# An LSTM with residual on one core: another assignment of hidden units to partitions, x and output in 16-step blocks, and a reordered setup

## The chip, the cores and the metric

The kernel runs on one core of a Trainium2 chip. The core has a matrix engine (PE, with its weight loads as PEld), a vector engine (DVE), an activation engine (ACT), a general engine (POOL) and a queue engine (SP). SP, ACT and POOL can issue DMA transfers, and sixteen DMA engines carry them out. The metric is the device time of one execution in microseconds (us).

## The reference

An LSTM over T = 512 steps for N = 16 sequences, with D = H = 512. All tensors are float32.

```
xW = einsum("ntd,dg->ntg", x, Wx) + b          # Wx is 512 x 2048
a  = xW[:, t] + h @ Wh                         # Wh is 512 x 2048
i, f, o = sigmoid(a[:, :512]), sigmoid(a[:, 512:1024]), sigmoid(a[:, 1024:1536])
g  = tanh(a[:, 1536:])
c  = f * c + i * g
h  = o * tanh(c)
out[:, t] = x[:, t] + h
```

`h` starts as `cond_1024` and `c` as zero. Every step needs the `h` of the step before.

## The kernel before, in words

**Layout.** The 512 hidden units (and the 512 inputs) are spread over 128 partitions and four chunks. Partition 32j+u and chunk c hold unit 128j+32c+u. So a 128-wide row of x for one (sequence, step) lies in group j as 128 consecutive floats, and a weight row for partition 32j+u and chunk c is row 128j+32c+u of `Wh` or `Wx`. PE works in four column groups j at once: each matmul writes 32 partitions of a PSUM bank, and the right side is a view of the weights (`wx_j`, `wh_j`, `wq_j`, lines 100 to 102) that picks for group j the columns of its 128 units in each of the four gates.

**Setup (lines 339 to 487).** `load_w` (line 128) loads `Wh` by DMAs of 32 partitions x 2 rows of 8 KB, half of them from SP's queue and half from ACT's; then SP issues the first x block and the start state, POOL issues the bias row, the bias copies and half of `Wx`, and SP the other half. `Wh` is split into three half-precision parts `wq` so that the recurrent product can run in float16. `bound` (line 398) finds the largest magnitude for the scale, `scales` makes the scale, and `split(n, k)` works on eighths n of `Wh` in five stages k: on ACT the first part (k=0), the second (k=2) and the third (k=4), on DVE the two remainders (k=1, k=3). While the split runs, `turn_x` (line 162) transposes x for the first three pairs of steps on DVE, `project` (line 167) multiplies two of them by `Wx` on PE into the banks `xb`, sixteen matmuls with zero follow (line 480), and `seed` (line 178) copies a projection into the gate bank. `xb` holds four pairs; three banks get the bias by matmul before the loop, the fourth by `put_bias` in step 0.

**Loop (lines 489 to 523).** Each step issues on PE, in the order written in `STEP_PE`, twelve `products` (line 186; 96 float16 matmuls of 256 columns) and two calls of `project` for the pair after next (8 float32 matmuls of 512 columns, two passes each). DVE and ACT do the gates in the order of `STEP`. In step 0 `first_products` multiplies the start state by float32 `Wh`. Each engine runs its instructions in the order of the program, since all five are scheduled by hand; the order across engines comes from semaphores. x comes in blocks of XB = 8 steps by 8 DMAs on SP (`load_xs`, line 145; 16 partitions x 4 x 512 B each) into four buffers; `residual` (line 324) adds x on POOL, and `put` (line 315) writes a block of 8 steps with 8 DMAs on SP.

Of the kernel before, what the change touches and what calls it, by code (L numbers as in the profile page):

```python
# [7 lines left out]
FP = mybir.dt.float32  # L8
HP = mybir.dt.float16
I32 = mybir.dt.int32  # L10
AF = mybir.ActivationFunctionType
ALU = mybir.AluOpType
PSUM = bass.MemoryType.PSUM

P = 128
Q = 32
XB = 8
LO = 4096.0
# [13 lines left out]
def lstm_residual(ctx: ExitStack, tc: tile.TileContext, x, h0, wx, wh, b, out):  # L32
# [24 lines left out]


    nc = tc.nc
    N, T, D = x.shape  # L60
# [10 lines left out]
    XP = XB // S2  # L71
    NXB = 4
    assert D == H and NJ * Q == P and N == 16 and S2 == 2 and T % XB == 0 and NK == 4

    const = ctx.enter_context(tc.tile_pool(name="const", bufs=1))
    tmp = ctx.enter_context(tc.tile_pool(name="tmp", bufs=3))
    xsp = ctx.enter_context(tc.tile_pool(name="xsp", bufs=4))
    xtp = ctx.enter_context(tc.tile_pool(name="xtp", bufs=3))
# [20 lines left out]

    wx_j = wx_sb.rearrange("p c (g j w) -> p c j g w", g=G, j=NJ)  # L100
    wh_j = wh_sb.rearrange("p c (e g j h u) -> p c e h j g u", e=2, g=2, j=NJ, h=2)
    wq_j = [w.rearrange("p c (g j h u) -> p c h j g u", g=G, j=NJ, h=2) for w in wq]
    bias = const.tile([P, G * P], FP, tag="bias", name="bias")
    mask = const.tile([P, S2], FP, tag="mask", name="mask")
    zero = const.tile([1, G * P], HP, tag="zero", name="zero")
    amax = const.tile([P, NK], FP, tag="amax", name="amax")
    top = const.tile([P, 2], FP, tag="top", name="top")
# [19 lines left out]

    def load_w(dst, w, c0, dmas, parts=1):


        n = G * H // parts
        for j in range(2):
            for q, dma in enumerate(dmas):
                r = w[(2 * q + j) * P + c0 * Q :][: 2 * Q].rearrange("(c u) f -> u c f", u=Q)
                p = slice((2 * q + j) * Q, (2 * q + j + 1) * Q)
                for e in range(parts):
                    a = parts - 1 - e
                    dma.dma_start(  # L138
                        out=dst[p, c0 : c0 + 2, a * n : (a + 1) * n],
                        in_=r[:, :, e * n : (e + 1) * n],  # L140
                    )

    xs = {}

    def load_xs(s, dma=nc.sync):

        xs[s] = xsp.tile([P, XP, P], FP, tag="xs", name=f"xs_{s}")
        for j in range(NJ):
            for r in range(S2):
                p0 = j * Q + r * N  # L150
                dma.dma_start(
                    out=xs[s][p0 : p0 + N],
                    in_=x[:, s * XB + r : (s + 1) * XB : S2, j * P : (j + 1) * P],
                )

# [6 lines left out]
    def turn_x(q):  # L162
        s, i = divmod(q, XP)
        xT[q] = xtp.tile([P, NK, Q], FP, tag="xT", name=f"xT_{q}")
        nc.vector.transpose(xT[q].rearrange("p c m -> p (c m)"), xs[s][:, i])

    def project(q, c):
        for j in range(NJ):
            nc.tensor.matmul(  # L169
                xb[q % NXB][j * Q : (j + 1) * Q],  # L170
                lhsT=xT[q][:, c],
                rhs=wx_j[:, c, j],
                start=False,
                stop=(c == NK - 1),
                skip_group_check=True,
            )
# [137 lines left out]

    def put(s, i0, i1, dmas):
        for j in range(NJ):
            for r in range(S2):
                p0 = j * Q + r * N
                dmas[r % len(dmas)].dma_start(
                    out=out[:, s * XB + S2 * i0 + r : s * XB + S2 * i1 : S2, j * P : (j + 1) * P],  # L320
                    in_=ob[s][p0 : p0 + N, i0:i1],
                )

    def residual(p):
        s, i = divmod(p, XP)
        if i == 0:
            ob[s] = outp.tile([P, XP, P], FP, tag="ob", name=f"ob_{s}")
        hb = work.tile([P, P], FP, tag="hb", name=f"hb_{p}")
        nc.vector.transpose(hb, hs[p].rearrange("p c m -> p (c m)"))  # L329
        nc.gpsimd.tensor_tensor(ob[s][:, i], hb, xs[s][:, i], ALU.add)  # L330
        if p == NP - 1:
            put(s, i, i + 1, [nc.sync, nc.scalar])
        elif p == NP - 2:
            put(s, 0, i + 1, [nc.sync])
        elif i == XP - 1:
            put(s, 0, XP, [nc.sync])

# [5 lines left out]
    ones = const.tile([1, Q], FP, tag="ones", name="ones")  # L343
    for c in (0, 2):
        load_w(wh_sb, wh, c, (nc.sync, nc.scalar))
    load_xs(0)
    nc.vector.memset(zero, 0.0)
    nc.vector.memset(h_in, 0.0)
    nc.vector.memset(ones, 1.0)
    for j in range(NJ):  # L350
        nc.sync.dma_start(out=h_in[j * Q : j * Q + N], in_=h0[:, j * P : (j + 1) * P])
    nc.gpsimd.dma_start(out=brow, in_=b.rearrange("(o f) -> o f", o=1))
    b_j = b.rearrange("(o e g j w) -> j e o g w", o=1, e=2, g=2, j=NJ)
    for j in range(NJ):
        for e in range(2):
            nc.gpsimd.dma_start(
                out=bias[j * Q : (j + 1) * Q, (1 - e) * GU : (2 - e) * GU].rearrange(
                    "p (g w) -> p g w", g=2
                ),
                in_=b_j[j, e].broadcast_to([Q, 2, P]),  # L360
            )
    for c in (0, 2):
        load_w(wx_sb, wx, c, (nc.sync, nc.gpsimd), 2)
    load_xs(1)
# [7 lines left out]
    for h in range(2):  # L372
        for i in range(2):
            nc.gpsimd.memset(parts[h][i], 0.0)
    nc.scalar.activation(warm, mask[0:1, 0:1], AF.Sigmoid)
# [7 lines left out]

    for bank in gates[0] + gates[1] + xb[3:]:
        zeros(bank, True)
    for bank in xb[:3]:
        for e in range(2):
            for j in range(NJ):
                nc.tensor.matmul(
                    bank[j * Q : (j + 1) * Q, (1 - e) * GU : (2 - e) * GU],  # L390
                    lhsT=ones,
                    rhs=brow.rearrange("p (e g j w) -> p e j g w", e=2, g=2, j=NJ)[:, e, j],
                    start=(e == 0),
                    stop=False,
                    skip_group_check=True,
                )

    def bound(c):
        if c == 1:
            junk = tmp.tile([P, G * H], HP, tag="junk", name="junk", bufs=1)  # L400
            nc.scalar.activation(junk, wh_sb[:, c], AF.Abs, accum_out=amax[:, c : c + 1])
        else:
            nc.vector.tensor_reduce(
                amax[:, c : c + 1],
                wh_sb[:, c],
                mybir.AxisListType.X,
                ALU.max,
                apply_absolute_value=True,
            )

    def scales(h):


        nc.vector.tensor_tensor(
            top[:, h : h + 1], amax[:, 2 * h : 2 * h + 1], amax[:, 2 * h + 1 : 2 * h + 2], ALU.max
        )
# [13 lines left out]
    def split(n, k):  # L430
# [18 lines left out]

    NH = 2 * NK  # L450
    bound(0)
    bound(1)
    scales(0)
# [3 lines left out]
    for n in range(NH):  # L457
        if n == 0:
            bound(2)
        if n == 2:  # L460
            bound(3)
            scales(1)
        if n + 1 < NH:
# [5 lines left out]
        if n + 2 < NH:  # L469
            split(n + 2, 0)  # L470
        if n == 3:
            for q in range(3):
                turn_x(q)
            nc.vector.transpose(hT0.rearrange("p c m -> p (c m)"), h_in)
        if n == 4:
            for c in range(NK):
                for q in range(2):
                    project(q, c)

            for _ in range(16):  # L480
                zeros(xb[3], False)
        if n == 6:
            for h in range(2):
                seed(0, h)
    split(NH - 1, 4)
    for h in range(2):
        seed(1, h)

    for t in range(T):
# [25 lines left out]
        else:  # L515
            if q + 1 < NP:
                put_bias(q + 1)
# [35 lines left out]
```

## Time and profile before

| | us |
|---|---|
| three runs | 2282.47, 2284.65, 2285.02 (median 2284.65) |
| the profiled execution's own time | 2284.45 |
| its span, first to last instruction | 2282.3 |
| first gate transpose of step 0 (DVE, L228) starts | 57.06 |
| distance from one step to the next in the loop | 4.34 |

A profile line gives the source line, the engine, the operation and the tiles (written <- read) with the number of instructions. In a timeline the first two numbers are the start and the length in us; what stands in brackets is how long the engine was idle before and what ended the idle time. In the table by stretches of time the DMA share is the mean busy share of the sixteen DMA engines (a share slightly over 1 means that their packets overlap), followed by GB/s. PE's instructions are counted twice for float32, as two passes.

### The profile page before, as it was taken

To read this page: it belongs to the slowest core of one execution; us is meant where nothing else is said; L and a number is where in the kernel's file an instruction comes from. 1 tells how busy PE (TensorE), PEld (TensorE's weight loads), DVE (VectorE), ACT (ScalarE), POOL (GpSimd) and SP (SyncE) were. 2 spreads that over 40 slices of the span, in tenths; PEclk is the share of its full clock that TensorE was granted. 3 is DMA by queue.
4 is the path that set the end of the run, shared out by engine and by line. 5 is a ranking of instruction groups with operands and counts; after the bars stand their busy time and mean duration, and the time that the engine had idled before them with its cause. 6 is when DMAs were issued, how large, how long until landed. Compare 5 with 4: busy or idle time off the path is not lost.

```text
span 2282.3 us, 137224 instructions
## 1 busy us (share of the span) xinstructions
PE 2239.7 (98%) x57445; PEld 1515.8 (66%) x57445; DVE 1952.7 (86%) x11813; ACT 1839.5 (81%) x7959; POOL 126.7 (6%) x281
## 2 busy tenths in 40 slices
PE   4999999999999999999999999999999999999997
PEld 2666666666666666666666666666666666666665
DVE  5888888888888888888888888888888888888887
ACT  5888888888888888888888888888888888888887
POOL 1000000000000000000000000000000000000000
PEclk9999999999999999999999999999999999999999
DMA  7000100101001001001001001010010010000000
GB/s 167 13 18 18 22 16 20 22 13 22 22 13 22 21 15 22 18 17 22 16 20 22 14 21 23 13 22 22 14 23 19 16 22 17 19 22 14 22 18 13
DMA packets 85004, 51.09 MB, mean 22 GB/s; under 512 B 17104, under 2 KB 82720, under 8 KB 83872
## 3 DMA queue, kind: packets, MB, share of 16 engines
q1 hardware_dynamic: 83008, 37.82, 7.7%
q8 instruction: 451, 7.39, 1.4%
q0 software_dynamic: 928, 2.37, 0.5%
q10 hardware_dynamic: 448, 2.13, 0.4%
q14 instruction: 169, 1.38, 0.2%
HBM read 25.47 MB, written 16.78 MB: 19 GB/s over the span
## 4 chain that ended last, share of the span: by engine, by line
PE 98%; DMA 2%; DVE 0%; issue 0%; ACTq 0%; POOLq 0%; POOL 0%; SPq 0%
PE gates L192 59%; PE xb L169 39%; DMA wh_sb<-in_L_cond_Wh_dram 1%; DMA xs<-in_x_dram 0%; DMA wx_sb<-in_L_cond_Wx_dram 0%; PE gates L205 0%; PE xb L378 0%; ACTq L138 0%; DVE gt L228 0%; DVE preo L235 0%; DVE pre L235 0%; DVE parts L288 0%; DVE gto L228 0%; POOLq L548 0%; POOL ob L330 0%
## 5 line engine op out<-in xcount | busy, mean ns | idle before, releaser
L192 PEld LDWEIGHTS <-parts 128*32 128x32 f16 x49056 | 1265.0, 96 | 397.6 <-DVE parts L288 300.7
L192 PE MATMUL gates<-wq,parts 128*32 128x256 f16 x49056 | 1428.1, 273 | 4.2 <-DVE parts L288 4.2
L169 PE MATMUL xb<-wx_sb,xT 128*32 128x512 f32 x8192 | 969.5, 593 | 22.5 <-DMA wx_sb<-in_L_cond_Wx_dram 22.5
L228 DVE STREAM_TRANSPOSE gt<-gates 128x192 f32<-128x192 f32 x1024 | 391.9, 383 | 220.0 <-PE gates L192 158.4
L169 PEld LDWEIGHTS xb<-wx_sb,xT 128*32 128x32 f32 x8192 | 240.9, 110 | 344.7 <-issue 319.6
L179 ACT ACTIVATE gates<-xb,mask 128x256 f32<-128x256 f32 x1024 | 450.9, 441 | 2.4 <-PE xb L169 2.4
L262 ACT ACTIVATE gc<-pre 128x32 f32<-128x32 f32 x1022 | 234.4, 229 | 260.0 <-DVE pre L235 247.7
L270 ACT ACTIVATE os<-so,sc 128x32 f32<-128x32 f32 x1024 | 329.3, 322 | 16.7
L292 ACT COPY parts<-parts 128x32 f16<-128x32 f16 x1022 | 214.6, 210 | 131.8 <-DVE parts L288 131.8
L235 DVE SCALAR_TENSOR_TENSOR pre<-gt 128x96 f32<-128x96 f32 x1024 | 253.4, 247 | 0.0
L264 ACT ACTIVATE sif<-pre 128x64 f32<-128x64 f32 x1024 | 245.0, 239 | 0.0
L330 POOL TENSOR_TENSOR ob<-hb,xs 128x128 f32<-128x128 f32 x256 | 116.6, 455 | 2136.9 <-DVE hb L329 1816.5
L228 DVE STREAM_TRANSPOSE gto<-gates 128x64 f32<-128x64 f32 x1024 | 229.8, 224 | 0.0
L280 ACT ACTIVATE tch<-gc 128x32 f32<-128x32 f32 x1024 | 227.0, 222 | 0.2
L268 ACT ACTIVATE so<-preo 128x32 f32<-128x32 f32 x1024 | 226.6, 221 | 0.0
L302 DVE SCALAR_TENSOR_TENSOR parts<-rem,parts 128x32 f16<-128x32 f32 x1022 | 196.1, 192 | 35.5
L235 DVE SCALAR_TENSOR_TENSOR preo<-gto 128x32 f32<-128x32 f32 x1024 | 192.2, 188 | 17.4
L294 DVE SCALAR_TENSOR_TENSOR parts<-parts,hist 128x32 f16<-128x32 f16 x1022 | 191.5, 187 | 17.8
L272 DVE TENSOR_TENSOR pr<-sif,gc 128x64 f32<-128x64 f32 x1022 | 204.3, 200 | 0.0
L288 DVE TENSOR_TENSOR parts<-os,tch 128x32 f16<-128x32 f32 x1022 | 196.6, 192 | 0.0
L278 DVE TENSOR_TENSOR gc<-pr 128x32 f32<-128x32 f32 x1024 | 191.8, 187 | 0.0
L282 DVE SCALAR_TENSOR_TENSOR hist<-os,tch 128x32 f32<-128x32 f32 x1024 | 188.5, 184 | 0.3 <-ACT tch L280 0.3
(47 smaller groups left out, 735.9 us busy)
## 6 DMA issues: line engine op xcount, KB each, us to landing
xs<-in_x_dram SPq DMA_DIRECT2D x512, 32.0 KB, 2.0
out_dram<-ob SPq DMA_DIRECT2D x504, 32.0 KB, 1.7
wh_sb<-in_L_cond_Wh_dram ACTq DMA_DIRECT2D x4, 512.0 KB, 13.2
wh_sb<-in_L_cond_Wh_dram SPq DMA_DIRECT2D x4, 512.0 KB, 12.8
wx_sb<-in_L_cond_Wx_dram POOLq DMA_DIRECT2D x8, 256.0 KB, 9.4
wx_sb<-in_L_cond_Wx_dram SPq DMA_DIRECT2D x8, 256.0 KB, 7.3
bias<-in_L_cond_b_dram POOLq DMA_DIRECT2D x8, 32.0 KB, 13.2
out_dram<-ob SPq DMA_DIRECT2D x8, 24.0 KB, 1.6
```

Of the source, the lines that this page charges most:

```text
L169: nc.tensor.matmul(xb[q % NXB][j * Q : (j + 1) * Q], lhsT=xT[q][:, c], rhs=wx_j[:, c, j], start=False, stop=(c == NK - 1), skip_group_chec ...
L179: nc.scalar.mul(gates[h][t % 2][:, :GU].rearrange("p (g u) -> p g u", g=G), xb[t // 2 % NXB].rearrange("p (g h u) -> p h g u", g=G, h=2)[: ...
L192: nc.tensor.matmul(g[j * Q : (j + 1) * Q, :GU], lhsT=a[:, cc, k * N : (k + 2) * N], rhs=wq_j[i - 1][:, 2 * kh + cc, h, j], start=False, st ...
L228: nc.vector.transpose(gt.rearrange("p b m -> p (b m)"), gates[h][t % 2][:, b0 * Q : b1 * Q])
L235: nc.vector.scalar_tensor_tensor(pre.rearrange("p g (c n) -> p (g c) n", c=2), gt[:, :, (1 - t % 2) * N : (2 - t % 2) * N], 1.0 / LO, gt[: ...
L262: nc.scalar.activation(gc[h][:, 0], v["pre", h][:, 0], AF.Tanh)
L264: nc.scalar.activation(new("sif", t, h, [P, 2, 2 * N]), v["pre", h][:, 1:3], AF.Sigmoid)
L268: nc.scalar.activation(new("so", t, h, [P, 2 * N]), v["preo", h][:, 0], AF.Sigmoid)
L270: nc.scalar.mul(new("os", t, h, [P, 2 * N]), v["so", h], S[h])
L272: nc.vector.tensor_tensor(new("pr", t, h, [P, 2, 2 * N]), v["sif", h], gc[h], ALU.mult)
L280: nc.scalar.activation(new("tch", t, h, [P, 2 * N]), gc[h][:, 1], AF.Tanh)
L292: nc.scalar.copy(slots(t, h, 2), slots(t, h, 0))
```

## The change

Partition 32j+u and chunk c now hold unit 128c+32j+u. A chunk of weights is then 128 consecutive rows over 128 partitions, a weight DMA covers 128 partitions x 4 KB, and x, the start state and the output move in runs of 32 floats (128 B) by (chunk, group, step parity). A block is 16 steps and takes 32 DMAs of 16 partitions x 8 x 128 B; x has three buffers. All weight DMAs are on SP. POOL loads the start state and the first three pairs of x. DVE reads one element of each x run (`seen`) before the first transpose of a block. ACT copies the bias bank into `bias` from a PSUM bank. The order of the setup changes, the zero matmuls of line 480 and `put_bias` in step 0 are gone, and the last `residual` adds on DVE.

```diff
-XB = 8
+XB = 16
+    FIRST = 3
-    xsp = ctx.enter_context(tc.tile_pool(name="xsp", bufs=4))
+    xsp = ctx.enter_context(tc.tile_pool(name="xsp", bufs=3))
...
-    wx_j = wx_sb.rearrange("p c (g j w) -> p c j g w", g=G, j=NJ)
-    wq_j = [w.rearrange("p c (g j h u) -> p c h j g u", g=G, j=NJ, h=2) for w in wq]
+    wx_j = wx_sb.rearrange("p k (g c j u) -> p k j g c u", g=G, c=NK, j=NJ)
+    wq_j = [
+        w.rearrange("p k (g h c j u) -> p k h j g c u", g=G, h=2, c=2, j=NJ) for w in wq
+    ]
...
+    def load_xs(s, i0=0):
+        if s not in xs:
+            xs[s] = xsp.tile([P, XP, P], FP, tag="xs", name=f"xs_{s}")
+        for c in range(NK):
+            for j in range(NJ):
+                for r in range(S2):
+                    p0 = j * Q + r * N
+                    nc.sync.dma_start(
+                        out=xs[s][p0 : p0 + N, i0:, c * Q : (c + 1) * Q],
+                        in_=x_j[j, :, s * XB + i0 * S2 + r : (s + 1) * XB : S2, c],
+                    )
+    def load_first(i1):
+        xs[0] = xsp.tile([P, XP, P], FP, tag="xs", name="xs_0")
+        for i in range(i1):
+            for j in range(NJ):
+                for r in range(S2):
+                    p0 = j * Q + r * N
+                    nc.gpsimd.dma_start(
+                        out=xs[0][p0 : p0 + N, i].rearrange("p (c u) -> p c u", c=NK),
+                        in_=x_j[j, :, i * S2 + r],
+                    )
...
     def turn_x(q):
         s, i = divmod(q, XP)
+        if i == 0 or q == FIRST:
+            a, e = (0, FIRST) if q == 0 else (i, XP)
+            seen = tmp.tile([P, XP, NK], FP, tag="seen", name=f"seen_{q}")
+            nc.vector.tensor_copy(
+                seen[:, a:e], xs[s].rearrange("p i (c u) -> p i c u", c=NK)[:, a:e, :, 0]
+            )
...
-        nc.gpsimd.tensor_tensor(ob[s][:, i], hb, xs[s][:, i], ALU.add)
+        add = nc.vector if p == NP - 1 else nc.gpsimd
+        add.tensor_tensor(ob[s][:, i], hb, xs[s][:, i], ALU.add)
...
-    for c in (0, 2):
-        load_w(wh_sb, wh, c, (nc.sync, nc.scalar))
-    load_xs(0)
+    nc.scalar.dma_start(out=brow, in_=b.rearrange("(o f) -> o f", o=1))
+    for c in range(NK):
+        for e in range(2):
+            f = slice(e * GH, (e + 1) * GH)
+            nc.sync.dma_start(out=wh_sb[:, c, f], in_=wh[c * P : (c + 1) * P, f])
...
-        nc.sync.dma_start(out=h_in[j * Q : j * Q + N], in_=h0[:, j * P : (j + 1) * P])
-    nc.gpsimd.dma_start(out=brow, in_=b.rearrange("(o f) -> o f", o=1))
+        nc.gpsimd.dma_start(
+            out=h_in[j * Q : j * Q + N].rearrange("p (c u) -> p c u", c=NK), in_=h0_j[j]
+        )
+    load_first(FIRST)
+    for c in range(NK):
         for e in range(2):
-            nc.gpsimd.dma_start(
...
-                in_=b_j[j, e].broadcast_to([Q, 2, P]),
-            )
-    for c in (0, 2):
-        load_w(wx_sb, wx, c, (nc.sync, nc.gpsimd), 2)
+            nc.sync.dma_start(
+                out=wx_sb[:, c, (1 - e) * GH : (2 - e) * GH],
+                in_=wx[c * P : (c + 1) * P, e * GH : (e + 1) * GH],
+            )
+    load_xs(0, FIRST)
     load_xs(1)
...
+    nc.scalar.copy(bias, xb[0])
...
-        if k == 0:
+        if k == 0 and n < 6:
             nc.scalar.mul(f[0], w, RS2[c // 2])
+        elif k == 0:
+            nc.vector.tensor_scalar(f[0], w, RS2[c // 2], None, ALU.mult)
...
-    bound(0)
-    bound(1)
+    bound(0, 0, False)
+    bound(1, 1, True, slice(0, GH))
+    bound(2, 1, False, slice(GH, 2 * GH))
     scales(0)
...
     for n in range(NH):
-        if n == 0:
-            bound(2)
+        if n == 1:
+            bound(3, 2, False)
+            bound(4, 3, True)
+            scales(1)
         if n == 2:
-            bound(3)
-            scales(1)
+            for q in range(FIRST):
+                turn_x(q)
+            nc.vector.transpose(hT0.rearrange("p c m -> p (c m)"), h_in)
+            for q in range(2):
+                for c in range(NK):
+                    project(q, c)
...
-        if n == 3:
-            for q in range(3):
-                turn_x(q)
-            nc.vector.transpose(hT0.rearrange("p c m -> p (c m)"), h_in)
-        if n == 4:
-            for c in range(NK):
-                for q in range(2):
-                    project(q, c)
-            for _ in range(16):
-                zeros(xb[3], False)
-        if n == 6:
-            for h in range(2):
-                seed(0, h)
+        if n == 5:
+            for t in range(2):
+                for h in range(2):
+                    seed(t, h)
     split(NH - 1, 4)
-    for h in range(2):
-        seed(1, h)
...
-            if q + 1 < NP:
+            if t and q + 1 < NP:
                 put_bias(q + 1)
```

In `bound(i, c, on_act, f)` the second argument is the chunk, the third the engine, and `f` the columns. `put` writes a block by 32 DMAs in the same form as `load_xs`. In the last block each pair is written by `put_pair` as soon as it is done, with 8 DMAs of 16 partitions x 4 x 128 B.

More of the change, by code (lines that the diff above doesn't have):

```diff
@@ L98, in lstm_residual @@
     wq = [const.tile([P, NK, G * H], HP, tag=f"wq{i}", name=f"wq{i}") for i in range(3)]
-    wx_j = wx_sb.rearrange("p c (g j w) -> p c j g w", g=G, j=NJ)
-    wh_j = wh_sb.rearrange("p c (e g j h u) -> p c e h j g u", e=2, g=2, j=NJ, h=2)
-    wq_j = [w.rearrange("p c (g j h u) -> p c h j g u", g=G, j=NJ, h=2) for w in wq]
+    wx_j = wx_sb.rearrange("p k (g c j u) -> p k j g c u", g=G, c=NK, j=NJ)
+    wh_j = wh_sb.rearrange(
+        "p k (e g h c j u) -> p k e h j g c u", e=2, g=2, h=2, c=2, j=NJ
+    )
+    wq_j = [
+        w.rearrange("p k (g h c j u) -> p k h j g c u", g=G, h=2, c=2, j=NJ) for w in wq
+    ]
     bias = const.tile([P, G * P], FP, tag="bias", name="bias")
@@ L105, in lstm_residual @@
     zero = const.tile([1, G * P], HP, tag="zero", name="zero")
-    amax = const.tile([P, NK], FP, tag="amax", name="amax")
+    amax = const.tile([P, 5], FP, tag="amax", name="amax")
     top = const.tile([P, 2], FP, tag="top", name="top")
@@ L126, in lstm_residual @@
     xb = [psum.tile([P, G * P], FP, tag=f"xb{i}", name=f"xb{i}") for i in range(NXB)]
[L128 to L140, printed above, removed]
-                    )
[L143 to L153, printed above, removed]
-                )
+    x_j = x.rearrange("n t (c j u) -> j n t c u", c=NK, j=NJ)
+    out_j = out.rearrange("n t (c j u) -> j n t c u", c=NK, j=NJ)
+    h0_j = h0.rearrange("n (c j u) -> j n c u", c=NK, j=NJ)
+    xs = {}
+    def load_xs(s, i0=0):
[8 more added lines that the diff above has]
+                        in_=x_j[j, :, s * XB + i0 * S2 + r : (s + 1) * XB : S2, c],
+                    )
+    def load_first(i1):
[8 more added lines that the diff above has]
+                    )
     xT = {}
@@ L173, in project @@
                 start=False,
-                stop=(c == NK - 1),
+                stop=False,
                 skip_group_check=True,
@@ L313, in unscale, with put, put_pair @@
         nc.scalar.mul(hs[p][:, a], hist[p // XP][:, p % XP, a], RSL[h])
-    def put(s, i0, i1, dmas):
+    def put(s):
+        for c in range(NK):
+            for j in range(NJ):
+                for r in range(S2):
+                    p0 = j * Q + r * N
+                    nc.sync.dma_start(
+                        out=out_j[j, :, s * XB + r : (s + 1) * XB : S2, c],
+                        in_=ob[s][p0 : p0 + N, :, c * Q : (c + 1) * Q],
+                    )
+    def put_pair(s, i, dmas):
         for j in range(NJ):
@@ L319, in put @@
                 dmas[r % len(dmas)].dma_start(
-                    out=out[:, s * XB + S2 * i0 + r : s * XB + S2 * i1 : S2, j * P : (j + 1) * P],
-                    in_=ob[s][p0 : p0 + N, i0:i1],
+                    out=out_j[j, :, s * XB + S2 * i + r],
+                    in_=ob[s][p0 : p0 + N, i].rearrange("p (c u) -> p c u", c=NK),
                 )
@@ L329, in residual @@
         nc.vector.transpose(hb, hs[p].rearrange("p c m -> p (c m)"))
-        nc.gpsimd.tensor_tensor(ob[s][:, i], hb, xs[s][:, i], ALU.add)
+        add = nc.vector if p == NP - 1 else nc.gpsimd
+        add.tensor_tensor(ob[s][:, i], hb, xs[s][:, i], ALU.add)
         if p == NP - 1:
-            put(s, i, i + 1, [nc.sync, nc.scalar])
-        elif p == NP - 2:
-            put(s, 0, i + 1, [nc.sync])
+            put_pair(s, i, [nc.sync, nc.scalar])
+        elif s == NS - 1:
+            put_pair(s, i, [nc.sync])
         elif i == XP - 1:
-            put(s, 0, XP, [nc.sync])
+            put(s)
     h_in = work.tile([P, P], FP, tag="h_in", name="h_in", bufs=1)
@@ L350, in lstm_residual @@
     for j in range(NJ):
-        nc.sync.dma_start(out=h_in[j * Q : j * Q + N], in_=h0[:, j * P : (j + 1) * P])
-    nc.gpsimd.dma_start(out=brow, in_=b.rearrange("(o f) -> o f", o=1))
-    b_j = b.rearrange("(o e g j w) -> j e o g w", o=1, e=2, g=2, j=NJ)
-    for j in range(NJ):
-        for e in range(2):
[L356 to L359, printed above, removed]
-                in_=b_j[j, e].broadcast_to([Q, 2, P]),
-            )
-    for c in (0, 2):
-        load_w(wx_sb, wx, c, (nc.sync, nc.gpsimd), 2)
+        nc.gpsimd.dma_start(
[3 more added lines that the diff above has]
+    for c in range(NK):
+        for e in range(2):
+            nc.sync.dma_start(
+                out=wx_sb[:, c, (1 - e) * GH : (2 - e) * GH],
+                in_=wx[c * P : (c + 1) * P, e * GH : (e + 1) * GH],
+            )
+    load_xs(0, FIRST)
     load_xs(1)
@@ L373, in lstm_residual @@
         for i in range(2):
-            nc.gpsimd.memset(parts[h][i], 0.0)
+            nc.vector.memset(parts[h][i], 0.0)
     nc.scalar.activation(warm, mask[0:1, 0:1], AF.Sigmoid)
@@ L380, in zeros @@
         )
-    for bank in gates[0] + gates[1] + xb[3:]:
+    for bank in gates[0] + gates[1]:
         zeros(bank, True)
-    for bank in xb[:3]:
+    for bank in xb:
         for e in range(2):
@@ L391, in lstm_residual @@
                     lhsT=ones,
-                    rhs=brow.rearrange("p (e g j w) -> p e j g w", e=2, g=2, j=NJ)[:, e, j],
+                    rhs=brow.rearrange("p (e g c j u) -> p e j g c u", e=2, g=2, c=NK, j=NJ)[
+                        :, e, j
+                    ],
                     start=(e == 0),
@@ L396, in lstm_residual, with bound @@
                 )
[L398 to L401, printed above, removed]
+    nc.scalar.copy(bias, xb[0])
+    def bound(i, c, on_act, f=slice(0, G * H)):
+        w = wh_sb[:, c, f]
+        if on_act:
+            junk = tmp.tile([P, G * H], HP, tag="junk", name=f"junk_{i}", bufs=1)
+            nc.scalar.activation(junk[:, f], w, AF.Abs, accum_out=amax[:, i : i + 1])
         else:
             nc.vector.tensor_reduce(
-                amax[:, c : c + 1],
-                wh_sb[:, c],
+                amax[:, i : i + 1],
+                w,
                 mybir.AxisListType.X,
@@ L411, in scales @@
     def scales(h):
-        nc.vector.tensor_tensor(
-            top[:, h : h + 1], amax[:, 2 * h : 2 * h + 1], amax[:, 2 * h + 1 : 2 * h + 2], ALU.max
+        nc.vector.tensor_reduce(
+            top[:, h : h + 1], amax[:, 3 * h : 3 + 2 * h], mybir.AxisListType.X, ALU.max
         )
@@ L457, in lstm_residual @@
     for n in range(NH):
-        if n == 0:
-            bound(2)
+        if n == 1:
+            bound(3, 2, False)
+            bound(4, 3, True)
+            scales(1)
         if n == 2:
-            bound(3)
-            scales(1)
+            for q in range(FIRST):
+                turn_x(q)
+            nc.vector.transpose(hT0.rearrange("p c m -> p (c m)"), h_in)
+            for q in range(2):
+                for c in range(NK):
+                    project(q, c)
         if n + 1 < NH:
```

## The prediction

> **What bounds the kernel now.** I read first the busy shares, then the stretches of time, the chain of waits, and the timeline of the setup. In the stretch from 104.40 on, PE is busy for all of 2155.60 us:
>
> ```profile
> 104.40:2260.00 2155.60, 2155.60 (x55676) 1464.43 (x55672) 1868.72 (x11431) 1759.79 (x7704) 113.41 (x249) 1.00 0.09 19
> ...
> L192 PE MATMUL gates<-wq,parts 128*32 128x256 f16 x49056 | 1428.1, 273 | 4.2 <-DVE parts L288 4.2
> L169 PE MATMUL xb<-wx_sb,xT 128*32 128x512 f32 x8192 | 969.5, 593 | 22.5 <-DMA wx_sb<-in_L_cond_Wx_dram 22.5
> ```
>
> The step is 2.62 us of products and 1.72 of projection, 4.34, and 511 such steps are 2216 of the 2282.3 us. So the change can gain in only two places, the setup before 57 us and the last microseconds; in the loop it can only lose, unless the matmuls themselves become faster. The setup, from the chain of waits, the waits of DVE in the timeline, and the stretches:
>
> ```profile
> 22.15 8.97 DMA xs<-in_x_dram
> 31.14 6.55 DMA wx_sb<-in_L_cond_Wx_dram
> 37.83 9.55 PE xb L169 x64
> 47.38 4.64 PE xb L378 x16
> 52.02 5.84 PE gates L205 x128
> ...
> 21.97 2.29 DVE L403 TENSOR_REDUCE amax<-wh_sb 128x1 f32<-128x2048 f32 x1 [4.08 <-DMA wh_sb<-in_L_cond_Wh_dram]
> 57.06 0.38 DVE L228 STREAM_TRANSPOSE gt<-gates 128x192 f32<-128x192 f32 x1 [7.45 <-PE gates L205]
> ...
> 7.00:12.40 5.40, 2.42 (x24) 1.32 (x28) 0.00 (x0) 0.00 (x0) 0.88 (x2) 1.00 1.04 247
> 31.00:37.80 6.80, 0.00 (x0) 0.00 (x1) 6.73 (x17) 5.70 (x6) 0.00 (x0) 1.00 1.04 211
> ```
>
> The last part of `Wx` lands at 37.8; from there PE needs 9.55 (two pairs, its first groups at half speed), 4.64 (zeros), 5.84 (first products, whose first half ends 0.8 before the last). DVE and ACT have their split done at 50.7. The DMA engines are fully busy to 37.8, at 203 to 247 GB/s. I count everything against the first gate transpose, 57.06.
>
> **The change part by part.** *Zeros gone:* 4.64 us on that chain. They keep PE busy, and PE would otherwise go from projection straight to the first products, so nothing is late for it.
>
> *Weights over 128 partitions.* Bounds for the rate: 239 GB/s, the row of `Wh` before (32 partitions per DMA), and 341, which the Trainium skill ("DMA: Bandwidth & Descriptors", Bandwidth) measured for 1 MB over 128 partitions. The same page (The descriptor swizzle) gives each engine its own memory port in a 128-partition transfer; the row shows engines that are busy and move only 247/16 = 15 GB/s each, as if they shared something. By the row `Wx` ends at 3.2 + 8.6 MB/239 = 39.2 us (3.2: the first data at 2.2 and 1 to complete; 8.6 MB: both weights and three pairs of x), by the page at 28.4. I take 300 GB/s, between them: 31.9. `Wh` chunk 1 is then there at 3.2 + 2.1/0.3 = 10.2; with its second bound (half of 2.28) and the scale (0.6) the split starts at 11.9, not 15.4.
>
> *PE's tail after `Wx`.* Pair 0 goes first, so that after the last quarter of `Wx` PE owes one quarter of pair 0 (two groups at 0.85, cold), pair 1 (four groups at 0.85 and four at 0.43: 5.1) and 5.9 of first products: with 0.1 to start and 0.8 off for the half, gate transpose = `Wx` + 12.0, so 43.9 at 300 GB/s. A gain of 13.2, if nothing else is late.
>
> *x and the start state on POOL's queue: the step that I think decides.* DVE reads `seen` for pairs 0 to 2 in the middle of the split, and everything of DVE behind it waits for POOL's 28 small DMAs (4 + 24). Small DMAs on that queue are slow while weights flow:
>
> ```profile
> 1.95 3.71 POOL L356 DMA_DIRECT2D bias<-in_L_cond_b_dram  x7
> 10.12 0.53 POOL L356 DMA_DIRECT2D bias<-in_L_cond_b_dram  x1 [4.47 <-DMA brow<-in_L_cond_b_dram]
> 12.05 0.53 POOL L138 DMA_DIRECT2D wx_sb<-in_L_cond_Wx_dram  x1 [1.39 <-DMA bias<-in_L_cond_b_dram]
> 13.63 0.53 POOL L138 DMA_DIRECT2D wx_sb<-in_L_cond_Wx_dram  x1 [1.05 <-DMA bias<-in_L_cond_b_dram]
> 15.97 0.53 POOL L138 DMA_DIRECT2D wx_sb<-in_L_cond_Wx_dram  x1 [1.81 <-DMA bias<-in_L_cond_b_dram]
> 17.54 0.53 POOL L138 DMA_DIRECT2D wx_sb<-in_L_cond_Wx_dram  x1 [1.03 <-DMA bias<-in_L_cond_b_dram]
> 19.51 0.53 POOL L138 DMA_DIRECT2D wx_sb<-in_L_cond_Wx_dram  x1 [1.45 <-DMA bias<-in_L_cond_b_dram]
> 21.61 1.72 POOL L138 DMA_DIRECT2D wx_sb<-in_L_cond_Wx_dram  x3 [1.57 <-DMA bias<-in_L_cond_b_dram]
> ```
>
> After eight DMAs POOL waits for the first to land (about 10 us), and then each issue waits for one more: one per 1.9 us, while two other queues (SP, ACT) move `Wh`; when `Wh` is in (21.8), three go without a wait. The change leaves one weight queue, so I halve it: 0.85 us each after a first landing at 9, T = 9 + 27 x 0.85 = 32. Ends: POOL's own 0.53 per issue gives T = 24; a full 1.9 until `Wx` is in (12 more by 32) and 0.53 for the other 16 gives 40.5.
>
> Behind `seen` (0.2) stand three transposes and the start state's (0.96), five k=1 at 1.24, six k=3 at 1.2 and two k=0: about T + 16 on DVE. The seeds on ACT need DVE's stage (4,3) at T + 8.5, the parts (4,4) and four seeds of 0.41: T + 11.2; first products to T + 17.1, gate transpose at **T + 16.4**. With T = 32 that is 48.4, a gain of 57.06 - 48.4 = **8.6**. POOL's wait decides if T > 27.5; DVE without it would be there at 22.4.
>
> *Split work moved:* ACT gives two k=0 (1.13 each) to DVE. No row shows this form; bounds 1.28 (the row of k=1, two sources) and 0.6 ("VectorE: DVE Perf Modes", What auto-detection actually checks: one source in SBUF can run at two elements per cycle). I take 0.65; the upper end takes 1.3 off the gain.
>
> *Bias copy on ACT, 0.6; memsets on DVE instead of POOL:* before 8 us, where ACT idles 8.2 and DVE 10.4 for `Wh`; if that cover were gone they would cost 1 us.
>
> *Rest of x block 0, behind both weights on SP.* `seen` at the end of step 1 (about 56) waits for its 32 DMAs: eight in flight, the others after `Wx` at 0.52: 32 + 24 x 0.55 + 2 = 47. About 9 us of cover; blocks 1 and 2 follow at 17 us each and are needed at 95 and later.
>
> *Blocks of 16 steps.* SP issues 64 DMAs per 69.4 us instead of 32. Before, eight take 4.1 to 4.9. Twice the runs per DMA: an issue of 16 runs (start state) lasts 0.33, of 64 runs 0.42, so 128 runs 0.55, and 64 x 0.65 = 42 us. The queue row gives 7.7% of 16 x 2282 us over its packets:
>
> ```profile
> q1 hardware_dynamic: 83008, 37.82, 7.7%
> ```
>
> 34 ns a packet. Afterwards each engine has 576 per block: 20 us. The page's Specifications speak against the change: under 512 B a transfer is read, modified and written. Taken as a doubling, my estimate is 39 us of 69.4. By either, the wait is hidden: a block of x has 27 steps from issue to use, the output buffer 18. If SP passed 69.4 us per block, each microsecond over would cost 32. The `seen` copies, 33 at 0.2, go on DVE just before its wait for PE (0.35 idle in odd steps): 0; at most 6.6.
>
> *Shorter runs for PE*, 32 columns instead of 64 (float16) or 128 (float32). A group of four products takes 2.62/24 = 109.2 ns for 256 columns, a projection group 430 for 2 x 512. If the time over a plain rate were per run, these two (four runs each) allow up to 0.57 ns a run; if it is per matmul, the rate is 0.418 ns a column and 2.3 ns remain. "TensorE: Matmul & The Clock Gate" (Wait — 56ns, not 53.3ns?) has it fixed per matmul, about 2.5. So 0, with 0.57 as the other end: 24 x 4 + 4 x 12 = 144 more runs a step, 82 ns, 42 us in all.
>
> *End:* the last add on DVE saves about 0.25 of POOL's 0.45, but the last output waits behind eight DMAs on SP as before: 0, within 0.5.
>
> **Sum.** The profiled execution took 2284.45, of which 2282.3 is span. Less 8.6: 2275.9; the median of the runs shown is 0.2 above that execution, so **2276**.
>
> **The rivals.** *A, x in time* (T under 28): `Wx` decides, or the split; gain 11 to 17, time about 2271. For it: POOL has its queue free from 1 us, and 128-byte runs are little data. Against: the 1.9 us per small DMA above. *C, x behind the weights* (T 36 to 44): gain 4.6 to -3.4, at 40.5 just 0.2: 2284.2, no change. For it: if the turn between queues goes by whole DMAs. *D, slower: PE pays per run.* At one column's time (0.418) per extra run, 60 ns a step, 31 us: 2276 + 31 = 2307. It decides from (8.6 + 4.6)/511/144 = 0.18 ns a run. Against it: the page, and that one constant per matmul fits both forms.
>
> **How the numbers follow.** Likeliest case 0.42 (gain 5 to 11, so 2273.5 to 2279.5), A 0.28, C 0.17, D 0.10, and 0.03 for T beyond 45, slower too. 0.2% is 4.6 us, about what a measurement of this kernel can tell from no change. Faster 0.42 + 0.28 = 0.70, same 0.17, slower 0.13. The range 2269 to 2285 leaves out D, the late end of C and the best of A (341 GB/s and T = 24 give 2268), about 0.2.
>
> **What would show it.** Right: no zeros between the projection and the first products, `Wx` landed near 32, DVE waiting in `seen` for x until about 32, the first gate transpose near 48, and 4.34 us per step. If DVE doesn't wait there, A; if beyond 38, C. A step over 4.36 us or PE waiting in the loop would be D or a loop that I misread; a wait at step 1's `seen` would mean x block 0 is later than 56.

## The result

| | before | after |
|---|---|---|
| median of six runs, us | 2284.46 (2282.21 to 2285.02) | 2270.79 (2268.74 to 2271.31) |
| span of the profiled execution | 2282.3 | 2268.2 |
| first gate transpose | 57.06 | 42.26 |
| third gate transpose (step 2) | 65.84 | 52.40 |

A step has two gate transposes, one for each half of the units. Only the first of each step is counted here, so the third is that of step 2.

The ratio of the times is 0.9942, 95% interval 0.9929 to 0.9954: the change makes the kernel faster by 13.7 us. That is inside the stated range, with the forecast sign, but it is the time of rival A (2271) and not of the likeliest case (2276).

The weights and the wait for x, in the stretches of time and in the timeline of the changed kernel (in the stretches the last three columns are the granted clock, called PEclk, the DMA share and GB/s):

```profile
2.00:7.00 5.00, 5.00 (x43) 2.04 (x45) 1.08 (x6) 1.37 (x3) 3.77 (x8) 1.00 0.86 282
7.00:12.40 5.40, 3.05 (x32) 0.99 (x24) 3.35 (x8) 1.15 (x2) 3.33 (x7) 1.00 1.03 391
12.40:17.00 4.60, 0.00 (x0) 0.00 (x0) 3.63 (x7) 4.24 (x5) 3.04 (x7) 1.00 1.03 374
17.00:22.00 5.00, 0.00 (x0) 0.00 (x0) 4.86 (x11) 5.00 (x7) 3.81 (x8) 1.00 1.04 376
22.00:27.00 5.00, 0.00 (x0) 0.00 (x0) 0.70 (x2) 2.80 (x3) 0.00 (x0) 1.00 0.88 299
27.00:32.00 5.00, 4.54 (x32) 1.38 (x36) 5.00 (x9) 2.77 (x3) 0.00 (x0) 1.00 0.13 20
...
45.00:50.00 5.00, 5.00 (x109) 3.41 (x104) 3.04 (x19) 2.55 (x12) 0.00 (x0) 0.75 0.18 27
```

```profile
12.26 0.15 DVE L456 TENSOR_SCALAR sc<-bits 128x1 f32<-128x1 f32 x1
...
26.96 0.17 DVE L179 COPY seen<-xs 128x12 f32<-128x12 f32 x1 [4.30 <-DMA xs<-in_x_dram]
...
27.45 8.52 PE L187 MATMUL xb<-wx_sb,xT 128*32 128x512 f32 x64 [17.41 <-DMA xs<-in_x_dram]
...
36.54 3.70 PE L223 MATMUL gates<-wh_sb,hT 128*32 128x128 f32 x128 [0.57 <-ACT gates L197]
...
39.92 2.42 DVE L481 TENSOR_TENSOR r<-r,wq 128x1024 f32<-128x1024 f32 x2
...
42.26 0.38 DVE L246 STREAM_TRANSPOSE gt<-gates 128x192 f32<-128x192 f32 x1
...
44.78 4.10 PE L210 MATMUL gates<-wq,parts 128*32 128x256 f16 x96 [2.83 <-DVE parts L306]
48.06 0.38 DVE L246 STREAM_TRANSPOSE gt<-gates 128x192 f32<-128x192 f32 x1 [1.73 <-PE gates L210]
...
52.40 0.38 DVE L246 STREAM_TRANSPOSE gt<-gates 128x192 f32<-128x192 f32 x1
...
2259.84 0.38 DVE L246 STREAM_TRANSPOSE gt<-gates 128x192 f32<-128x192 f32 x1 [0.32 <-PE gates L210]
```

The DMA engines are done with the weights at about 27 instead of 37.8. DVE waits 4.30 us in `seen` for x and has its split done at 42.34 (39.92 + 2.42); the first products have ended at 40.24, so the first gate transpose at 42.26 comes straight behind DVE's own last split work, without a wait for PE. For step 1 and the loop, the same lines of the kernel before:

```profile
59.40 2.92 PE L192 MATMUL gates<-wq,parts 128*32 128x256 f16 x96
...
65.84 0.38 DVE L228 STREAM_TRANSPOSE gt<-gates 128x192 f32<-128x192 f32 x1 [0.35 <-PE gates L192]
...
2273.26 0.38 DVE L228 STREAM_TRANSPOSE gt<-gates 128x192 f32<-128x192 f32 x1 [0.32 <-PE gates L192]
```

From the third gate transpose to the last one the kernel before takes 2273.26 - 65.84 = 2207.42 us and the changed one 2259.84 - 52.40 = 2207.44: the loop costs the same. The span's 14.1 are thus 14.80 at the first gate transpose, less 1.36 that the first two steps lose (48.06 to 52.40 is a normal step of 4.34, but 42.26 to 48.06 is 5.80, before it was 4.45; 1.18 of the 1.36 are step 1's products, 4.10 instead of 2.92), plus 0.68 after the last gate transpose (9.04 before, 8.36 after).

### The profile page after: what moved, and what is told of

Its sections match the earlier page's. It is cut to its first block, busy times and chain, and to the rows that moved or that the text cites. A ratio compares the mean times of both kernels' runs of the same rounds, so it can differ in the third digit from the quotient of the medians.

```text
span 2268.2 us, 138001 instructions
## 1 busy us (share of the span) xinstructions
PE 2234.5 (99%) x57444; PEld 1466.8 (65%) x57444; DVE 1957.2 (86%) x11853; ACT 1839.7 (81%) x7959; POOL 131.1 (6%) x287
## 3 DMA queue, kind: packets, MB, share of 16 engines
q1 hardware_dynamic: 295872, 41.85, 11.4%
## 4 chain that ended last, share of the span: by engine, by line
PE 97%; DMA 1%; DVE 1%; issue 0%; ACT 0%; POOL 0%; SPq 0%; POOLq 0%; DVEq 0%
PE gates L210 59%; PE xb L187 38%; DMA xs<-in_x_dram 1%; DVE r L481 0%; DMA h_in<-in_cond_dram 0%; DVE r L474 0%; ACT wq L483 0%; SPq L347 0%; POOL h_in L382 0%; DMA out_dram<-ob 0%; DVE wq L471 0%; DVE xT L183 0%; POOLq L578 0%; DVE pr L290 0%; POOL ob L359 0%
## 5 line engine op out<-in xcount | busy, mean ns | idle before, releaser
L210 PEld LDWEIGHTS <-parts 128*32 128x32 f16 x49056 | 1224.7, 96 | 442.2 <-DVE parts L306 306.0
L187 PEld LDWEIGHTS xb<-wx_sb,xT 128*32 128x32 f32 x8192 | 235.4, 110 | 344.1 <-issue 340.3
```

Source lines behind the costliest of these rows:

```text
L187: nc.tensor.matmul(xb[q % NXB][j * Q : (j + 1) * Q], lhsT=xT[q][:, c], rhs=wx_j[:, c, j], start=False, stop=False, skip_group_check=True,)
L210: nc.tensor.matmul(g[j * Q : (j + 1) * Q, :GU], lhsT=a[:, cc, k * N : (k + 2) * N], rhs=wq_j[i - 1][:, 2 * kh + cc, h, j], start=False, st ...
```

## The experiments

The theory that the runs test: DVE's wait for POOL's small DMAs, and then the split, set the end of the setup, and PE's chain lies beside it. The rivals: the weights and PE's chain set it, or the zeros' removal is most of the gain.

**The zeros, in the kernel before.**

```diff
-            for _ in range(16):
-                zeros(xb[3], False)
```

> The kernel before, without its sixteen zero matmuls. Theory 1 (the zeros stand on PE's chain, as the prediction has it): the first gate transpose moves from 57.06 to about 52.4, the time falls by 4.6 to about 2279.9. Theory 2 (the zeros also run with a falling granted clock, so that the first products behind them take 5.84 us and not the 3.70 of the changed kernel): first products take about 3.7, the first gate transpose is near 50.7, where the split ends on ACT, and the time falls by 6 or more. Theory 3 (they keep PE fast): first products take longer than 5.84 and the gain is under 3.

Measured: 2277.75 against 2282.11 for the kernel before beside it, ratio 0.9978 (0.9968 to 0.9988). The timeline:

```profile
47.26 3.68 PE L205 MATMUL gates<-wh_sb,hT 128*32 128x128 f32 x128
...
50.13 0.38 DVE L228 STREAM_TRANSPOSE gt<-gates 128x192 f32<-128x192 f32 x1 [0.45 <-PE gates L205]
```

The first gate transpose comes 6.9 earlier, the third (59.43) 6.4. Theory 2 for the trace: the first products also shrink from 5.84 to 3.68. The medians differ by only 4.4, less than the 6 of theory 2: the times of the kernel before lie in two groups (see the last experiment), and its trace is from the upper one.

**The zeros, in the changed kernel**, put back behind the projection:

```diff
+            for _ in range(16):
+                zeros(xb[3], False)
```

> The changed kernel with the sixteen one-row zero matmuls put back between the projection and the first products. Theory 1 (their removal is worth in the changed kernel only what PE then passes DVE, which ends its split at 42.26): the first products start 4.6 us later, at about 41, and end at 45 to 47; the first gate transpose moves from 42.26 to 44 to 46, the third from 52.40 to 54 to 55.5, the time rises by 2 to 3.5. Theory 2 (they are worth as much here as in the kernel before, 6.4 at the third gate transpose): 5 to 7. Theory 3 (DVE hides them altogether): under 1.

Measured: 2270.65 (three runs), the time of the changed kernel (2270.79, in another session). The first gate transpose moves by 1.1, to 43.38, and the third not at all:

```profile
35.57 3.62 PE L407 MATMUL xb<-zero 1*128 1x512 f16 x16
...
39.12 5.37 PE L223 MATMUL gates<-wh_sb,hT 128*32 128x128 f32 x128
43.38 0.38 DVE L246 STREAM_TRANSPOSE gt<-gates 128x192 f32<-128x192 f32 x1 [1.41 <-PE gates L223]
...
46.03 2.80 PE L210 MATMUL gates<-wq,parts 128*32 128x256 f16 x96
...
52.34 0.38 DVE L246 STREAM_TRANSPOSE gt<-gates 128x192 f32<-128x192 f32 x1
```

Theory 3 for the time: in the changed kernel the removal is worth nothing. The zeros take 3.62 here, and the first products behind them are slower, at a granted clock of 0.57 from 40 to 44, so that they end 4.25 later (39.12 + 5.37 against 40.24). DVE's own work hides all of that but 1.1, and those come back in step 1, where PE is at full speed here (2.80 instead of 4.10). So the same edit that brings 6.4 us alone brings none beside the others: their gains don't add.

**The wait for x.** DVE waits in the split for two pairs and transposes the third two eighths later:

```diff
-        if i == 0 or q == FIRST:
+        if i == 0 or q in (2, FIRST):
-            a, e = (0, FIRST) if q == 0 else (i, XP)
+            a, e = (0, 2) if q == 0 else (2, FIRST) if q == 2 else (i, XP)
...
-            for q in range(FIRST):
+            for q in range(2):
...
+        if n == 4:
+            turn_x(2)
```

> The changed kernel, where DVE waits in the split only for pairs 0 and 1 of x (and the start state) and transposes pair 2 two eighths later: 20 of POOL's 28 small DMAs count. Theory 1 (POOL's x sets the setup's end, and behind it stands the rest of x block 0): the wait in the first seen copy falls from 4.30 us to under 1, the first gate transpose comes from 42.26 to 38 or 39, and then DVE waits about 4 us in the seen copy of step 1, which can't pass before the rest of the block has landed at about 52; the time stays within 1 us of the changed kernel's. Theory 2 (Wx and PE's chain set the end): the first gate transpose stays within 1 us of 42.3. Theory 3 (nothing stands behind it): the time falls by 3.5 to 5.

Measured: 2266.10 (2264.45 to 2267.58), 4.25 below `a_rest2` of the same session, which runs as the changed kernel does.

```profile
23.00 0.17 DVE L179 COPY seen<-xs 128x8 f32<-128x8 f32 x1
...
32.68 3.68 PE L223 MATMUL gates<-wh_sb,hT 128*32 128x128 f32 x128
...
38.24 0.38 DVE L246 STREAM_TRANSPOSE gt<-gates 128x192 f32<-128x192 f32 x1
...
40.77 4.38 PE L210 MATMUL gates<-wq,parts 128*32 128x256 f16 x96 [2.69 <-DVE parts L306]
...
48.27 0.18 DVE L179 COPY seen<-xs 128x20 f32<-128x20 f32 x1 [0.18 <-DMA xs<-in_x_dram]
```

The 4.30 are gone, the first gate transpose comes 4.02 earlier and the third, at 48.78, 3.62: x's wait did set the end. The second half of theory 1 fails: no wait appears in step 1. The 0.18 that the changed kernel also has there is no late transfer, as it stays 0.18 when DVE arrives 3.7 us earlier. Theory 3.

**The rest of x block 0**, half of its DMAs on POOL; first alone, then with the edit above:

```diff
-                    nc.sync.dma_start(
+                    (nc.gpsimd if i0 and r else nc.sync).dma_start(
```

> The changed kernel, where half of the 32 DMAs for the rest of x block 0 are issued by POOL, behind the first three pairs, and half by SP. Theory 1: the rest has landed before 48 (SP issues 16 DMAs fewer, 0.55 each), the seen copy of step 1 doesn't wait, but that wait was only 0.18 us; the first gate transpose stays at 42.3 and the time within 1 us. Theory 3: the same.

Measured: 2270.35 (2269.34 to 2271.08), no change, as both theories had it.

> Both edits together. Theory 1: first gate transpose at 38 to 39, no wait over 0.5 us at the seen copy of step 1, PE's first loop products no longer at half speed (4.10 us to about 2.6), time 3.5 to 5 us below the changed kernel's. Theory 2 (Wx and PE set the end): gain under 1.5 us.

Measured: 2266.84 (2265.78 to 2267.76), the gain of `a_first2` and no more. First gate transpose at 37.14, but step 1's products still take 4.13, not 2.6. In both kernels DVE is idle 0.57 before step 1's `seen`, where it was 0.18 with all 32 DMAs on one queue. Since earlier x doesn't shorten it and a second queue makes it longer, it looks like the taking of the waits itself; that is argued, not shown.

**What sets the pace of POOL's small DMAs.** `Wh` on two queues:

```diff
-            nc.sync.dma_start(out=wh_sb[:, c, f], in_=wh[c * P : (c + 1) * P, f])
+            (nc.sync, nc.scalar)[e].dma_start(out=wh_sb[:, c, f], in_=wh[c * P : (c + 1) * P, f])
```

> The changed kernel with Wh's eight DMAs issued half by SP and half by ACT; all of Wx stays on SP. Theory 1 (the pace of POOL's small DMAs is set by how many queues move weights, the halving in the prediction): while Wh flows a small DMA lands every 1.4 us or more and not every 0.7, the first seen copy starts 5 us or more after 27.0, and the time rises by as much. Theory 2 (the pace follows the data, not the number of queues): the first seen copy stays within 1.5 us of 27.0 and the time within 2 us of the changed kernel's.

Measured: 2271.39 (two runs) and `seen` at 28.36, 1.4 later, since the first small DMA lands 1.7 later (POOL's ninth starts at 9.50 instead of 7.80). While the weights flow (377 to 387 GB/s from 7 to 22), POOL issues one per 0.7 us:

```profile
13.45 0.51 POOL L162 DMA_DIRECT2D xs<-in_x_dram  x1 [0.18 <-issue]
...
14.15 0.51 POOL L162 DMA_DIRECT2D xs<-in_x_dram  x1 [0.19 <-issue]
...
15.07 0.51 POOL L162 DMA_DIRECT2D xs<-in_x_dram  x1 [0.41 <-DMA xs<-in_x_dram]
15.77 0.51 POOL L162 DMA_DIRECT2D xs<-in_x_dram  x1 [0.19 <-issue]
16.49 0.51 POOL L162 DMA_DIRECT2D xs<-in_x_dram  x1 [0.20 <-issue]
```

Theory 2: the number of queues doesn't set it; ACT's queue moves weights until 16.6 here. The first gate transpose is 1.4 later too (43.65), the third only 0.2 (52.61): step 1's products take 2.91 here, at a granted clock of 1.00, after a wait of 2.44 us.

**The 128 partitions.** `Wh` by 32 partitions, all else as changed:

```diff
-    for c in range(NK):
-        for e in range(2):
-            f = slice(e * GH, (e + 1) * GH)
-            nc.sync.dma_start(out=wh_sb[:, c, f], in_=wh[c * P : (c + 1) * P, f])
+    for c in (0, 2):
+        for j in range(NJ):
+            nc.sync.dma_start(
+                out=wh_sb[j * Q : (j + 1) * Q, c : c + 2],
+                in_=wh.rearrange("(c j u) f -> j u c f", c=NK, j=NJ)[j, :, c : c + 2],
+            )
```

> The changed kernel with Wh loaded by eight DMAs of 32 partitions x 2 rows of 8 KB (512 KB each, as many as before it, all on SP); Wx stays as it is. Theory 1 (the rate comes from covering 128 partitions): between 2 and 12 us the DMAs move 240 GB/s or less, the scale is ready 2 us or more after 12.4, all weights are in 5 to 8 us later, and the time rises by 3 to 8. Theory 2 (the rate comes from one queue, or from the order): the rate stays at 280 to 390 GB/s and the time within 1.5 us.

Measured: 2276.70 (2276.22 to 2278.05), 5.9 above the changed kernel (in another session); the third gate transpose at 58.78, 6.4 later. The stretches of this kernel:

```profile
2.00:7.00 5.00, 3.94 (x31) 1.72 (x33) 0.43 (x5) 1.40 (x3) 3.77 (x8) 1.00 0.96 206
7.00:12.40 5.40, 4.18 (x40) 1.80 (x32) 0.00 (x0) 0.00 (x0) 1.76 (x4) 1.00 1.01 202
12.40:17.00 4.60, 0.00 (x0) 0.00 (x0) 2.13 (x1) 1.15 (x2) 2.32 (x5) 1.00 1.03 209
17.00:22.00 5.00, 0.00 (x0) 0.00 (x0) 3.89 (x11) 2.73 (x3) 1.57 (x4) 1.00 1.03 209
...
27.00:32.00 5.00, 0.00 (x0) 0.00 (x0) 3.24 (x10) 5.00 (x6) 1.25 (x3) 1.00 1.05 374
```

```profile
18.77 0.15 DVE L458 TENSOR_SCALAR sc<-bits 128x1 f32<-128x1 f32 x1
...
19.81 0.51 POOL L162 DMA_DIRECT2D xs<-in_x_dram  x1 [0.54 <-DMA xs<-in_x_dram]
...
20.70 0.51 POOL L162 DMA_DIRECT2D xs<-in_x_dram  x1 [0.38 <-DMA xs<-in_x_dram]
...
21.97 0.51 POOL L162 DMA_DIRECT2D xs<-in_x_dram  x1 [0.76 <-DMA xs<-in_x_dram]
```

While `Wh` comes by 32 partitions the engines are as busy but move 202 to 209 GB/s; `Wx`, by 128, again 374. The instruction that makes the scale starts at 18.77 instead of 12.26. Theory 1. The edit also makes the rows 8 KB long instead of 4, but `Wx` of the kernel before came in rows of 4 KB by 32 partitions and moved 211 GB/s (31.00:37.80), so the row length is not what slows it. The first gate transpose is at 48.49 here, still 8.6 before 57.06; how those 8.6 divide between the other edits no run separates. POOL's small DMAs also pass more slowly here, about 1.2 us each between 13 and 24, so their pace goes with the weights' rate.

**The granted clock.** The zeros of the kernel before on 128 rows (`wide`, a zero tile of 128 partitions) instead of one:

```diff
-                zeros(xb[3], False)
+                wide_zeros(xb[3])
...
+    def wide_zeros(bank):
+        nc.tensor.matmul(
+            bank, lhsT=wide[:, :P], rhs=wide, start=False, stop=False, skip_group_check=True
+        )
```

> The kernel before with its sixteen zero matmuls on 128 rows instead of one (zero times zero, the same bank). Theory 1 (a matmul with one row lets the granted clock fall): the sixteen take 16 x 0.213 = 3.4 us instead of 4.64, the granted clock stays at 1.00 through the first products, these take 3.7 instead of 5.84, and the time falls by about 3.3 against before, less than the 6.8 of the span without the zeros. Theory 2 (the clock falls for another reason, such as the wait before): first products still take 5.5 or more and the time stays within 1.5 us of before.

Measured: the sixteen take 3.55 (47.14 to 50.69), the first products 3.70, the third gate transpose is at 62.37, 3.5 earlier. The column PEclk of the stretches, first this kernel, then the kernel before:

```profile
48.00:52.00 4.00, 4.00 (x61) 2.38 (x63) 1.23 (x1) 2.89 (x5) 0.00 (x0) 1.00 0.10 28
52.00:58.00 6.00, 6.00 (x176) 4.41 (x172) 3.64 (x22) 3.29 (x15) 0.00 (x0) 1.00 0.01 3
```

```profile
47.40:52.00 4.60, 4.60 (x20) 1.57 (x23) 1.23 (x1) 3.67 (x6) 0.00 (x0) 0.75 0.10 29
52.00:58.00 6.00, 6.00 (x133) 5.46 (x136) 0.84 (x5) 0.23 (x2) 0.00 (x0) 0.62 0.01 3
...
49.00:50.00 1.00, 1.00 (x5) 0.41 (x4) 0.62 (x1) 0.66 (x2) 0.00 (x0) 0.85 0.08 23
50.00:51.00 1.00, 1.00 (x4) 0.32 (x3) 0.00 (x0) 1.00 (x3) 0.00 (x0) 0.50 0.00 0
```

Both keep PE busy all the time; with one row in use the mean granted clock of the two stretches falls to 0.75 and 0.62, with 128 it stays at 1.00. These are means: in shorter stretches of the kernel before the clock is 1.00 up to 49, 0.85 in the next microsecond and 0.50 from 50 to 56. Theory 1 for the trace; numbers of rows between 1 and 128 were not tried. The times don't resolve it: 2280.43 against 2281.96, ratio 0.9991 (0.9982 to 1.0001).

Then the same for step 1 of the changed kernel: `a_first2` with ten such zeros where PE waited 2.69 us.

```diff
+        if t == 0:
+            for _ in range(10):
+                wide_zeros(xb[3])
```

> The changed kernel with DVE waiting for two pairs only, and ten 128-row zero matmuls on PE between step 0's projection and step 1's products, where PE waited 2.69 us for DVE. Theory 1 (PE's idle stretch is what makes step 1's products take 4.38 instead of 2.62): they take 2.7, the second gate transpose follows 4.5 us after the first and not 5.25, and the time is 0.7 to 1.7 below that of the same kernel without them (about 2265). Theory 2 (the clock falls because of the first products themselves): step 1's products stay above 4 us and the time at about 2266; if the ten delay PE, up to 1 more.

Measured: 2265.21 (2264.85 to 2265.82), ratio to before 0.9924 (0.9912 to 0.9936). Step 1's products take 2.80 at a granted clock of 1.00 (stretch 40.00:44.00) instead of 4.38, of which most ran at 0.50, and the third gate transpose is at 47.16, 1.6 before `a_first2`'s 48.78:

```profile
40.84 2.80 PE L211 MATMUL gates<-wq,parts 128*32 128x256 f16 x96
```

Theory 1 in the trace; between 2265.21 and 2266.10, of different sessions, the times can't tell. It is 5.6 below the changed kernel, and no version here has a lower median.

**The scatter of the kernel before.** Its times spread over 5 us, in two groups, while those of all variants spread less. It was run once more unchanged:

> The kernel before once more, to see why its times lie in two groups (2280.5 to 2282.2 and 2284.1 to 2285.6). Theory 1 (the granted clock falls during the one-row zeros in some executions and not in others): with a time near 2281 the granted clock is 1.00 in the zeros, these take about 3.5 and the first products 3.7, and the third gate transpose comes 3 to 4 us before 65.84; with a time near 2284.5 the profile is as shown before. Theory 2 (the groups come from somewhere else): with a time near 2281 the third gate transpose stays within 1 us of 65.84.

Measured: 2280.11 to 2284.95; the profiled execution took 2284.76 and looks like the one shown (granted clock 0.81 and 0.57 in the same two stretches). There is no profile of an execution near 2281, so neither theory is tested by a trace. The mean granted clock of whole executions speaks for theory 1: every recorded one of this kernel at 2284 or more has 0.998, every one below 2281.6 has 0.999, and with the zeros on 128 rows or taken out all have 0.999 and the upper group is gone. Which stretch was slow in each is not recorded, so the cause of the scatter stays open.

## Why the prediction was right, and where not

**The step that decides** was rightly named: the wait for x on POOL's queue, shown by `a_first2`. It was mis-sized. Foreseen T = 32, measured 26.96: the first landing near 7.8 instead of 9 (POOL's ninth DMA waits until then), then (26.96 - 7.8)/27 = 0.71 us each instead of 0.85. These 5 us are the larger part of why A's time came and not 2276. The condition given for A, T below 28, held, but A's mechanism did not: in A DVE doesn't wait and `Wx` or the split comes last, while here DVE waited 4.30 us and `a_first2` shows that wait to be worth 4.25. The bound "POOL's wait decides if T > 27.5" was too high, as it rested on `Wx` at 31.9 (43.9 - 16.4); with `Wx` in at about 27 the same sum gives 22.6. That the time fell on A's is thus in part chance. In numbers, the gain foreseen was 8.6; 5.04 from T, 1.1 from the way behind it and 0.68 at the end come on top, and 1.36 are lost in step 1, which makes the 14.1 of the span. The reason for the 0.85, one weight queue instead of two, was wrong: two queues leave 0.7 (`a_two_queues`), while a slower stream gives 1.2 (`a_part32`). The 1.9 that was halved also came from bias DMAs of 32 KB each, and those of x have 8 KB; what the size adds no run separates. What is shared in detail stays open.

**From T to the gate transpose**: foreseen T + 16.4, measured T + 15.3. But the end was set by DVE (foreseen T + 16, measured T + 15.4) and not by PE, whose first products took 3.70, not 5.9, and were over at T + 13.3. I had carried 5.84 over from a stretch in which the clock was granted at 0.62, without reading that column. The DVE form of k=0 took 0.75 (foreseen 0.65, row of the two-source form 1.28).

**The zeros** were put at 4.64 on the chain. In the kernel before they cost 6.4 in the traces (4.4 in the medians), with their effect on the clock; in the changed kernel nothing. PE did go on almost at once, after 0.57 us for a seed, but PE no longer led.

**The rate of the weights**: taken at 300 GB/s between 239 and 341, measured 374 to 391 once it runs, so that the weights were in at about 27 and not at 31.9. The Trainium skill's 341 ("DMA: Bandwidth & Descriptors", Bandwidth) is for a single transfer of 1 MB; as the upper end for sixteen transfers one behind another it was too low. Its other statement used, that with 128 partitions each engine has a memory port of its own, fits `a_part32`'s 202 to 209 against 374; the ports themselves no run shows.

**The loop at no cost** held to 0.02 us in 2207. Shorter runs for PE cost nothing, so D falls, and the per-matmul reading of the Trainium skill's "TensorE: Matmul & The Clock Gate" (Wait — 56ns, not 53.3ns?) stands. For the DMAs, the queue's row:

```profile
q1 hardware_dynamic: 295872, 41.85, 11.4%
```

That is 0.114 x 16 x 2268.2 us over 295872, 14 ns a packet, where I had used 34 and feared twice that. So the skill's rule that transfers under 512 B are read, modified and written ("DMA: Bandwidth & Descriptors", Specifications) brings no doubling per packet here. The queue's share of the engines' time still rises from 7.7% to 11.4% for nearly the same bytes (37.82 and 41.85 MB), but it is hidden: outputs land in a median 1.6 us, before in 1.7. SP needs 37 to 39 us of 69.4 for its 64 DMAs (18.65 and 18.13 in one block, 20.01 and 19.34 in the next), foreseen 42. The rest of block 0 was in time.

**Not foreseen**: step 1 at reduced speed. PE idles 2.83 us for DVE, the granted clock is 0.50 from 44.78 to 47.5, and 1.36 us are lost. That the idle time brings the low clock is shown for `a_first2` by `a_first2_warm`. **The end**, called 0 within 0.5, gave 0.68; why was not tested.

## What to carry to other kernels

When several chains run side by side to one point, price a removal on each of them: the zeros were worth 6.4 us alone (4.4 in the medians) and nothing next to edits that left another engine last. Spread a load over all 128 partitions before splitting it over queues; small transfers that an engine waits for in program order should be few in the first wait, or be asked for later. Matmuls meant to keep PE's clock up should use all 128 rows, as those that worked here did. A duration taken from the trace is only good with the granted clock of its stretch beside it, and even that doesn't show everything: the changed kernel's first projection groups start 0.85 us apart and those from 30.64 on 0.43, with 1.00 in the column for both.

## What the runs showed of the hardware that I had not expected

Sixteen matmuls with one row, in sequence for 4.6 us, bring the granted clock down to 0.50 from 50 to 56; with 128 rows, also of zeros, it stays at 1.00, and the products behind them take 3.70 instead of 5.84 us. Waits of PE of 2.58 to 2.84 us were followed by a clock of 0.50 in step 1 (`a_rest2`, `a_both`, `a_first2`, the changed kernel, `a_part32`), one of 2.44 us was not (`a_two_queues`); with one trace each this gives no threshold. DMA engines with equal busy shares (1.03) moved 209 GB/s into 32 partitions per transfer and 374 into 128. SP's queue took 14 ns of an engine per packet with packets of mostly 128 B, and 34 before with mostly 512 B. Runs of 32 instead of 64 or 128 columns left the step at 4.34 us.
